# A hybrid convolution/attention network on one core: the bias table ahead of the first projection, filling products on the array, layer 1's weights prepared during the first image, and two edits in layer 1

## The chip, the core and the metric

The kernel runs on one core of a Trainium2 chip. The metric is the device time of one execution in microseconds. TensorE is called the array or PE here, VectorE DVE, ScalarE ACT, GpSimd POOL, and SyncE (which only issues transfers here) SP. ACT issues transfers too. Each engine takes its instructions in the order in which the program gives them, and each waits for what its own instructions need.

## The reference

Eight images of 384 channels and 32 x 32 positions (1024 tokens), all in float32, pass through two layers. Layer 0 is attention of 8 heads of 48 channels with a learnt bias for each relative position; layer 1 is attention of 6 heads of 64 channels and a feed-forward network with signed weights (computed for the first five images; the others get zero).

```python
# layer 0
rel = coords[:, None, :] - coords[None, :, :]          # over (31, 31)
hidden = gelu(rel @ mlp_w1 + mlp_b1)                   # 192 wide, exact gelu
bias = hidden @ mlp_w2 + mlp_b2                        # one per head and pair of positions
q, k, v = heads(groupnorm(x) @ qkv_w + qkv_b)
attn = softmax(q @ k.T * 48 ** -0.5 + bias)
x = x + (attn @ v) @ proj_w + proj_b
# layer 1
q, k, v = heads(layernorm(t) @ qkv_w.T)
q, k = normalize(q), normalize(k)                      # (t - mean) / std over a head's 64 channels
t = t + (softmax(q @ k.T * 64 ** -0.5) @ v) @ proj_w.T + proj_b
t = t + bitlinear(gelu(bitlinear(layernorm(t), W1, b1)), W2, b2)
```

The bias depends only on the difference of two positions, so 63 x 63 = 3969 values per head are all there is.

## The kernel before, in words

Everything is written out in program order by hand, image by image. Small pieces of work that are to run beside the main stream are given to a list (`later`): `later.after(n, work)` emits `work` after n further steps. In image 0 a step is taken after each of the six products of `project_qk` (three pairs of heads, q and k), after each of the four of `project_v`, and then after each of the 32 units of attention. So step 10 lies between the last product of `project_v` and unit 0.

**The order at the start.** `stages` are the pieces of the group norm of image 0: three measure the channels as they land and send the statistics to DRAM and back (`there`, `gs`), `stages[3]` makes scale and shift (`gsc`), `stages[4]` applies them on VectorE. `place_weights_qk` moves the q and k weights from a raw copy that lies in `grow` to their place. `hidden(r)` (r = 0, 1) makes the hidden layer of the bias network: four products `ph` of two rows each on the array (K = 2), each followed by a gelu on ACT. `table_part(r)` multiplies them by the second weights (`pb`, 16 records) and writes one half of the positions of the four groups to a table in DRAM (`table`). Before the change `table_part(0)` stands ahead of the first product of `project_qk`, and `table_part(1)` behind it.

**The bias parts.** `grow` holds the bias, spread out so that a score tile can read its own with one access pattern. It is filled in 32 parts, (head, quarter) in that order. `grow_loads` issues four transfers on SP for a part (`wide<-table`, or `oT<-table` for the parts from the 21st on, which use another buffer), 457 KB in all; `grow_turns` turns it round into `grow`, even quarters on ACT, odd ones on VectorE. The loads go out in lots of 3, 3, 3, 3, 2, 2, 2, 2 at steps 2 to 9, the turns at steps 3 to 6 and 8 to 11. So 18 turns stand ahead of unit 0 in the engines' queues, and one more comes at each step from 11 on. `wide` has the nine buffers of the tag `e`, which `rel` and the hidden tiles use first.

**A unit.** `scores` makes two tiles of scores on the array (L521, `s`), VectorE adds the bias to each (L532, "bias sum", two of 1.2 us), ACT takes the exponential (L536), and `weigh` multiplies by v two units later (L552, `o`). There are four PSUM tiles in all.

**Layer 1's first weights.** `_Start` loads them during image 7 of layer 0, takes the mean over the inputs with products of ones (`cm`, L146: 12 and 6 records), subtracts it on GpSimd, and then takes each head's mean out of q and k (`heads`).

**The end.** In the last image `divide` sums the exponentials of the last pair (`sum`, L1398), sends the sums through DRAM to spread them, inverts them and multiplies (L1434). `project_out` (`pp`, L1453) has done the first two pairs by then and waits for the third. Each third of the output is added on VectorE (L1458) and stored.

**Feed-forward images.** Behind attention the array makes the token sums `tsf` in the middle of the next image's first projection product, and `tsa` (the sums for the next image's norm) after it. `layer_norm` sends `lr` to DRAM and reads it back as `lc` and `ls`.

Of the kernel before, what the change touches and what calls it, by code (L numbers as in the profile page):

```python
# [19 lines left out]
F32 = mybir.dt.float32  # L20
# [100 lines left out]
class _Start:  # L121
# [4 lines left out]
    def __init__(self, tc, ins, x1, shared):  # L126
        self.nc, self.ins, self.x1, self.shared = tc.nc, ins, x1, shared

    def load_weights(self):
        self.wqkv = self.shared.weights("wqkv").rearrange("p (k c) -> p k c", k=KC)  # L130
        self.nc.sync.dma_start(
            self.wqkv, self.ins["L1_attn_qkv_wT"].rearrange("(k p) c -> p k c", p=P)
        )
# [5 lines left out]
    def means(self, temp, at, n):  # L139
        nc = self.nc  # L140
        pm = self.shared.mm2(f"cm{at}")
        for h in range(-(-n // HALF)):
            w = min(HALF, n - h * HALF)
            for k in range(KC):
                cols = slice(at + h * HALF, at + h * HALF + w)
                nc.tensor.matmul(  # L146
                    pm[:, h, :w], self.shared.ones, self.wqkv[:, k, cols],
                    start=(k == 0), stop=(k == KC - 1),
                )
        self.mean = temp(f"cmean{at}")  # L150
        nc.scalar.activation(
            self.mean[:, :n], pm.rearrange("p h q -> p (h q)")[:, :n], AF.Copy, scale=1.0 / C
        )

    def subtract(self, at, n):
        for k in range(KC):
            w = self.wqkv[:, k, at : at + n]
            self.nc.gpsimd.tensor_sub(w, w, self.mean[:, :n])

    def heads(self, k):  # L160
        nc = self.nc
        w = self.wqkv[:, k, 0 : 2 * C].rearrange("p (h d) -> p h d", d=D1)
        hm = self.shared.pool.tile([P, 2 * H1], F32, tag="hm", name=f"hm{k}")
        nc.vector.tensor_reduce(hm, w, AX.X, ALU.add)
        nc.gpsimd.tensor_scalar(hm, hm, 1.0 / D1, 1.0, ALU.mult, ALU.mult)
        nc.gpsimd.tensor_sub(w, w, hm.unsqueeze(2).to_broadcast([P, 2 * H1, D1]))

    def stages(self, temp):

        first, rest = (0, 2 * HALF), (2 * HALF, 3 * C - 2 * HALF)  # L170
        return [
            (5, self.load_weights),
            (6, self.load_image),
            (10, lambda: self.means(temp, *first)),
            (11, lambda: self.subtract(*first)),
            (12, lambda: self.means(temp, *rest)),
            (14, lambda: self.subtract(*rest)),
            (19, lambda: self.heads(0)),
            (21, lambda: self.heads(1)),
            (23, lambda: self.heads(2)),  # L180
        ]


def _layer0(tc, ins, x1, sums, shared, beside):
# [9 lines left out]
    with ExitStack() as ctx:  # L194
# [31 lines left out]
        QT, QN = 32, 2 * HALF  # L226
# [5 lines left out]
        nc.vector.memset(rel, 0.0)  # L232
        nc.vector.memset(w2, 0.0)
        nc.vector.memset(b2, 0.0)
        for g in range(P // QT):
            at = g * QN
            n = min(QN, NREL - at)
            nc.scalar.dma_start(rel[g * QT : g * QT + 2, 0:n], ins["rel"][:, at : at + n])
            nc.scalar.dma_start(w1[g * QT : g * QT + 2], ins["L0_conv_mlp_w1"])
        with nc.allow_non_contiguous_dma(reason="a bias, once"):  # L240
            nc.scalar.dma_start(b1, ins["L0_conv_mlp_b1"].rearrange("(k p) -> p k", p=HC))
            nc.scalar.dma_start(
                w2[:, :, 0:H0], ins["L0_conv_mlp_w2"].rearrange("(k p) h -> p k h", p=HC)
            )
        for g in range(P // QT):
            nc.scalar.dma_start(b2[g * QT : g * QT + H0], ins["L0_conv_mlp_b2"].unsqueeze(1))
# [8 lines left out]
        first = load(0)  # L255

# [31 lines left out]

        def place_weights_qk():
# [13 lines left out]
        def load_bias_qk():  # L303
            with nc.allow_non_contiguous_dma(reason="a bias, once"):
                for j in range(2):
                    for row, n, at, step in (
                        (j * S0, D0, j * D0, 2 * D0),
                        (j * S0 + D0, FR, (2 * NF0 + j) * D0, FR),
                    ):
                        for s in range(2):  # L310
                            nc.sync.dma_start(
                                bqk[row : row + n, s],
                                bass.AP(
                                    qkv_b.tensor, qkv_b.offset + s * C + at, [[1, n], [step, NF0]]
                                ),
                            )

        def load_weights_v_out():
            nc.sync.dma_start(wv, qkv_w[:, 2 * C : 3 * C].rearrange("(k p) c -> p k c", p=P))
            nc.sync.dma_start(bv, qkv_b[2 * C : 3 * C].partition_broadcast(P))  # L320
            pw = ins["L0_conv_proj_w"]
            for j in range(2):
                last = (2 * NF0 + j) * D0
                for row, n, at, step in (
# [3 lines left out]
                    nc.sync.dma_start(  # L328
# [5 lines left out]
                nc.sync.dma_start(wl[j * S0 + SP : (j + 1) * S0], pw[last : last + D0])  # L334
            with nc.allow_non_contiguous_dma(reason="a bias, once"):
                nc.sync.dma_start(bp, ins["L0_conv_proj_b"].rearrange("(k p) -> p k", p=P))
# [3 lines left out]
        WR = GW // 4  # L340

        def hidden(r):

            hids = {}
            for k in range(2):
                for a in range(2):
                    ph = mm2(f"ph{r}{k}{a}")
                    for i in range(2):
# [17 lines left out]
        def table_part(r, hids):  # L366
            pb = mm2(f"pb{r}")
            for k in range(2):
# [6 lines left out]
            nc.vector.tensor_scalar_add(backwards(part[:, HALF - 1 : HALF], HALF), pb[:, 0], b2)  # L375
            for g in range(P // QT):
                at = g * QN + r * HALF
                n = min(HALF, NREL - at)
# [264 lines left out]
        place_weights_qk()  # L643
        hids = [hidden(r) for r in range(2)]
        stages[3]()
        load_bias_qk()
        stages[4](nc.vector)
        load_weights_v_out()
        table_part(0, hids[0])
        later.after(1, lambda: table_part(1, hids[1]))  # L650
        nc.scalar.activation(tiny[:, 1:2], tiny[:, 0:1], AF.Exp)
# [14 lines left out]
        for i, n in enumerate((3, 3, 3, 3, 2, 2, 2, 2)):  # L666
            later.after(i + 3 + (i > 3), lambda n=n: grow_turns(n))
            later.after(i + 2, lambda n=n: grow_loads(n))
        for i in range(len(parts) - 20):
# [4 lines left out]
        with_last = beside(etile)  # L674
        for b in range(B):
            held = []
            for i, u in enumerate(units):
# [10 lines left out]
                if b == B - 1:  # L688
                    for at, work in with_last:
# [341 lines left out]
def _layer1(tc, ins, x1, out, shared, start, before=None, check=None):  # L1031
# [4 lines left out]
    with ExitStack() as ctx:  # L1036
# [405 lines left out]
        def project_out(b, oT, xt, then, between=None):  # L1442

            pps = []
            for pairs in (range(NP1 - 1), range(NP1 - 1, NP1)):
                if between is not None and NP1 - 1 in pairs:
                    between()
                for m in range(KC):
                    if len(pps) <= m:
                        pps.append(mm2(f"pp{b}_{m}"))  # L1450
                    for k in pairs:
                        for h in range(NH):
# [4 lines left out]
                    if NP1 - 1 in pairs:  # L1457
                        nc.vector.scalar_tensor_tensor(  # L1458
                            xt[:, m], flat2(pps[m]), bp[:, m : m + 1], xt[:, m], ALU.add, ALU.add
                        )  # L1460
                        then(m)

        def store(b, xt, k):
            nc.sync.dma_start(out[b, ts(k, P)].rearrange("p h w -> p (h w)"), xt[:, k])
# [404 lines left out]
```

## Time and profile before

| | |
|---|---|
| Median of three runs | 3040.62 us (3038.88 to 3041.24) |
| Profiled execution, its own time | 3043.66 us |
| Span of its instructions | 3041.8 us |
| PE / DVE / ACT / POOL busy | 3017.7 / 1769.1 / 1402.7 / 465.0 us |
| Mean granted clock of the array | 0.999 |
| Mean DMA rate | 49 GB/s |
| First product of `project_qk`, image 0 | 23.24 us |
| First scores, image 0 | 73.86 us |
| First product of `project_qk`, image 1 | 189.20 us |
| Last array record begins | in the group at 3029.19 us, 5.42 us long |

Times in the profile are microseconds from the start of the span. A line of the order of time gives start, length, engine, line of the program, operation, output<-input, shapes, how many were merged, and in brackets how long the engine was idle before and what ended it. A float32 product shows as two records. Rows of SPq or ACTq are issues of transfers, not the transfers. An array that is "busy" may still run at half its clock: the granted clock stands in the table by stretches, and the distance of records shows it as well.

### The profile page before, as it was taken

To read this page: it belongs to the slowest core of one execution; us is meant where nothing else is said; L and a number is where in the kernel's file an instruction comes from. 1 tells how busy PE (TensorE), PEld (TensorE's weight loads), DVE (VectorE), ACT (ScalarE), POOL (GpSimd) and SP (SyncE) were. 2 spreads that over 40 slices of the span, in tenths; PEclk is the share of its full clock that TensorE was granted. 3 is DMA by queue.
4 is the path that set the end of the run, shared out by engine and by line. 5 is a ranking of instruction groups with operands and counts; after the bars stand their busy time and mean duration, and the time that the engine had idled before them with its cause. 6 is when DMAs were issued, how large, how long until landed. Compare 5 with 4: busy or idle time off the path is not lost.

```text
span 3041.8 us, 45673 instructions
## 1 busy us (share of the span) xinstructions
PE 3017.7 (99%) x18914; PEld 1610.8 (53%) x18914; DVE 1769.1 (58%) x1760; ACT 1402.7 (46%) x1760; POOL 465.0 (15%) x315
## 2 busy tenths in 40 slices
PE   8999999999999999999999999999999999999998
PEld 3455546455554645444545655655655655645453
DVE  3746647373655727355565765765765755755545
ACT  2634526253443616244463553553653543654534
POOL 0111102021110202123202202202202202211110
PEclk9999999999999999999999999999999999999999
DMA  7412020211212020121411101101101101102011
GB/s 178 120 26 83 19 82 23 70 32 26 76 22 79 23 78 23 32 93 51 108 34 37 50 16 37 50 22 31 50 23 30 50 23 30 50 17 72 16 51 44
DMA packets 102449, 150.48 MB, mean 49 GB/s; under 512 B 59924, under 2 KB 63492, under 8 KB 101464
## 3 DMA queue, kind: packets, MB, share of 16 engines
q1 hardware_dynamic: 99368, 147.41, 17.3%
q8 instruction: 152, 2.49, 0.3%
q14 instruction: 65, 0.53, 0.1%
q10 hardware_dynamic: 2864, 0.05, 0.1%
HBM read 111.05 MB, written 27.32 MB: 45 GB/s over the span
## 4 chain that ended last, share of the span: by engine, by line
PE 93%; DMA 3%; DVE 3%; ACT 1%; SPq 1%; issue 0%; POOL 0%; ACTq 0%; DVEq 0%; POOLq 0%
PE s L521 15%; PE o L552 14%; PE s L1322 11%; PE o L1371 11%; PE pq L467 8%; PE pq L1178 6%; PE y2p L1593 6%; PE pp L616 4%; PE pv L1259 4%; PE y1p L1542 4%; PE pp L1453 4%; PE pv L495 4%; PE sum L1398 1%; DMA wide<-table 1%; PE hs L1207 1%; DVE lun L1494 1%
## 5 line engine op out<-in xcount | busy, mean ns | idle before, releaser
L536 ACT ACTIVATE e<-e 128x1024 f32<-128x1024 f32 x512 | 535.0, 1057 | 441.9 <-DVE e L532 422.0
L532 DVE TENSOR_TENSOR e<-s,grow 128x1024 f32<-128x1024 f32 x512 | 601.4, 1219 | 190.3 <-PE s L521 189.7
L521 PE MATMUL s<-qk 48*64 48x512 f32 x4096 | 613.5, 592 | 3.3 <-DVE e L532 3.2
L552 PE MATMUL o<-e,v 64*64 64x512 f32 x4096 | 607.5, 589 | 0.0
L1333 ACT ACTIVATE e<-s,kc 128x512 f32<-128x512 f32 x768 | 463.9, 694 | 172.2 <-PE s L1322 161.6
L1322 PE MATMUL s<-qk,qk 64*64 64x512 f32 x3072 | 418.6, 592 | 1.1 <-DVE oT L1381 0.9
L1371 PE MATMUL o<-e,v 64*64 64x512 f32 x3072 | 414.9, 590 | 0.0
L521 PEld LDWEIGHTS s<-qk 48*64 48x64 f32 x4096 | 237.4, 132 | 230.0 <-issue 76.7
L552 PEld LDWEIGHTS o<-e,v 64*64 64x64 f32 x4096 | 259.4, 133 | 178.5 <-issue 71.1
L1348 DVE TENSOR_TENSOR t<-t,e 128x1024 f32<-128x1024 f32 x192 | 231.0, 1222 | 53.4 <-ACT e L1333 53.3
L1178 PE MATMUL pq<-bx,wqkv 128*128 128x512 f32 x576 | 255.4, 596 | 0.7 <-ACT tra L1150 0.7
L1322 PEld LDWEIGHTS s<-qk,qk 64*64 64x64 f32 x3072 | 153.5, 132 | 191.5 <-issue 110.1
L467 PE MATMUL pq<-xn,w 128*128 128x512 f32 x576 | 251.6, 598 | 0.0
L1371 PEld LDWEIGHTS o<-e,v 64*64 64x64 f32 x3072 | 158.8, 133 | 169.9 <-issue 142.6
L581 POOL TENSOR_TENSOR inv<-sums,over 128x16 f32<-128x16 f32 x32 | 92.8, 2900 | 1009.7 <-DMA sums<-sd 851.0
L467 PEld LDWEIGHTS pq<-xn,w 128*128 128x128 f32 x576 | 109.5, 191 | 142.8 <-issue 140.3
L1178 PEld LDWEIGHTS pq<-bx,wqkv 128*128 128x128 f32 x576 | 107.4, 190 | 145.3 <-issue 141.5
L1345 DVE TENSOR_TENSOR t<-e,e 128x1024 f32<-128x1024 f32 x96 | 114.2, 1224 | 79.6 <-ACT e L1333 79.5
L1529 DVE TENSOR_REDUCE parts<-y 128x1 f32<-128x1024 f32 x75 | 90.1, 1217 | 93.3 <-ACT y L1526 92.7
L1228 POOL TENSOR_TENSOR hc<-hc,rsqrt 128x32 f32<-128x32 f32 x24 | 139.2, 5800 | 2.0
L1194 ACT ACTIVATE qsq<-pq 128x1024 f32<-128x1024 f32 x48 | 49.2, 1025 | 194.5 <-DVE qk L1188 105.8
L477 DVE TENSOR_SCALAR qk<-pq,bqk 128x1024 f32<-128x1024 f32 x24 | 30.8, 1284 | 177.1 <-PE pq L467 177.1
(161 smaller groups left out, 3026.9 us busy)
## 6 DMA issues: line engine op xcount, KB each, us to landing
rb<-rd SPq DMA_DIRECT2D x112, 256.0 KB
xn<-in_x_dram SPq DMA_DIRECT2D x24, 512.0 KB
res<-in_x_dram SPq DMA_DIRECT2D x24, 512.0 KB
x<-res SPq DMA_DIRECT2D x24, 512.0 KB
bx<-x SPq DMA_DIRECT2D x8, 1536.0 KB
rq<-hi SPq DMA_DIRECT2D x48, 256.0 KB
out_dram<-bx SPq DMA_DIRECT2D x24, 512.0 KB
wide<-table SPq DMA_DIRECT2D x80, 114.2 KB
```

Source lines behind the costliest of these rows:

```text
L467: nc.tensor.matmul(pq[:, h], wqk[:, k, s, 2 * pair : 2 * pair + 2, :].rearrange("p h d -> p (h d)"), xn[:, k, ts(h, HALF)], start=(k == 0) ...
L521: nc.tensor.matmul(s[j][ts(c, QP), i], qk[pair][rows, 1, ts(4 * m2 + 2 * i + c, QP)], qk[pair][rows, 0, ts(h, HALF)], start=True, stop=True,)
L532: nc.vector.tensor_add(e.rearrange("p (i q) -> p i q", i=2), s[j], bass.AP(near.tensor, near.offset, [near.ap[0], [-QROWS * IW, 2], [1, HA ...
L536: nc.scalar.activation(e, e, AF.Exp)
L552: nc.tensor.matmul(po[ts(j, S0), r], v[keys, 2 * m2 + i, 2 * pair + j, :], es[j][keys, ts(i, HALF)], start=(m2 == 0 and i == 0), stop=(m2 ...
L1178: nc.tensor.matmul(pq[:, h], wqkv[:, k, s * C + pair * P : s * C + (pair + 1) * P], xt[:, k, ts(h, HALF)], start=(k == 0), stop=(k == KC - 1),
L1228: nc.gpsimd.tensor_tensor(c, c, rsqrt.to_broadcast(list(c.shape)), ALU.pow)
L1322: nc.tensor.matmul(s[j][ts(c, QP), i], qk[pair, 1][rows, ts(4 * m2 + 2 * i + c, QP)], qk[pair, 0][rows, ts(h, HALF)], start=True, stop=True,)
L1333: nc.scalar.activation(e[:, ts(i, HALF)], s[j][:, i], AF.Exp, scale=kc[:, pair, j, m : m + 1])
L1348: nc.vector.tensor_add(total[j], total[j], e)
L1371: nc.tensor.matmul(po[ts(j, D1), r], v[keys, 2 * m2 + i, at : at + D1], es[j][keys, ts(i, HALF)], start=(m2 == 0 and i == 0), stop=(m2 == ...
L1593: nc.tensor.matmul(py[m][:, h], w2[:, k, ts(m, P)], supply.parts[k][i][:, ts(h, HALF)], start=(k == 0 and i == 0), stop=(k == FC - 1 and i ...
```

## The change

The change has three parts.

1. Image 0. Both table parts are emitted ahead of the first projection. The table's groups are 982, 982, 982 and 1023 positions wide instead of 1024, 1024, 1024 and 897, so `rel` and `w1` come in four transfers instead of eight and only one column of `rel` is cleared. `stir` puts products of ones into a free PSUM bank: seven ahead of the first `ph`, one ahead of each other `ph` and each `pb`, two behind the second `pb`. The second table part is evicted by ACT. `b1` is loaded by SP ahead of the raw weights, `w2` and `b2` by ACT after the gelu's table has been loaded by a tiny instruction. The biases of q and k and the weights for v and for the output move from SP's queue to ACT's, behind the table. The bias parts are loaded at steps 0 to 7 and turned at steps 2 to 5 and 7 to 10, so 20 turns stand ahead of unit 0. Layer 1's first weights come over ACT's queue into the room of the last three heads of `grow`; GpSimd adds their three chunks (step 2), three products of ones sum over the partitions (step 3), VectorE scales (step 4), GpSimd subtracts and takes out the heads' means (steps 4 to 8), and the result is stored to DRAM (step 9). In image 7 it is only loaded again.
2. The end. `divide_last` sums with 64 columns of ones, so that each partition of PSUM has its divisor; VectorE inverts from PSUM and multiplies. The last third of the output is added and stored in two halves. The loops of `project_out` over halves and pairs are exchanged.
3. `tsa` is emitted directly behind `tsf`.

```diff
+class _Weights:
+    def load(self, here, mean):
+        self.w = here.rearrange("p (k c) -> p k c", k=KC)
+        self.mean = mean
+        self.nc.scalar.dma_start(
+            self.w, self.ins["L1_attn_qkv_wT"].rearrange("(k p) c -> p k c", p=P)
         )
+    def add(self):
+        for k in range(1, KC):
+            self.nc.gpsimd.tensor_add(self.mean, self.w[:, 0] if k == 1 else self.mean, self.w[:, k])
+    def means(self):
...
+                self.nc.tensor.matmul(
+                    pm[:, h, :w], self.shared.ones, self.mean[:, cols], start=True, stop=True
+                )
...
+    def take(self):
+        for at, n, pm in self.sums:
+            self.nc.vector.tensor_scalar_mul(self.mean[:, at : at + n], pm[:, :n], 1.0 / C)
+    def subtract(self, k):
+        self.nc.gpsimd.tensor_sub(self.w[:, k], self.w[:, k], self.mean)
...
+    def store(self):
+        self.nc.sync.dma_start(self.ready, self.w.rearrange("p k c -> p (k c)"))
...
+        def stir(bank, n):
+            for _ in range(n):
+                nc.tensor.matmul(
+                    bank.rearrange("p (a b) -> p a b", b=P), shared.ones,
+                    shared.ones.unsqueeze(1).to_broadcast([P, HALF // P, P]), start=True, stop=True,
+                )
...
                     ph = mm2(f"ph{r}{k}{a}")
+                    stir(ph[:, 0], 1 if r or k or a else 7)
...
             pb = mm2(f"pb{r}")
+            stir(pb[:, 1], 1)
...
-            nc.vector.tensor_scalar_add(backwards(part[:, HALF - 1 : HALF], HALF), pb[:, 0], b2)
+            turned = backwards(part[:, HALF - 1 : HALF], HALF)
+            if r == 0:
+                nc.vector.tensor_scalar_add(turned, pb[:, 0], b2)
+            else:
+                stir(pb[:, 1], 2)
+                nc.scalar.activation(turned, pb[:, 0], AF.Identity, bias=b2)
...
         place_weights_qk()
+        nc.scalar.activation(tiny[:, 1:2], tiny[:, 0:1], AF.Gelu)
+        load_hidden_rest()
         hids = [hidden(r) for r in range(2)]
         stages[3]()
+        for r in range(2):
+            table_part(r, hids[r])
         load_bias_qk()
+        nc.scalar.activation(tiny[:, 1:2], tiny[:, 0:1], AF.Exp)
+        weights.load(*early)
+        load_weights_v_out()
         stages[4](nc.vector)
-        load_weights_v_out()
-        table_part(0, hids[0])
-        later.after(1, lambda: table_part(1, hids[1]))
-        nc.scalar.activation(tiny[:, 1:2], tiny[:, 0:1], AF.Exp)
+        for at, work in (
+            (2, weights.add), (3, weights.means), (4, weights.take), *(
+                (at + k, lambda k=k, work=work: work(k))
+                for at, work in ((4, weights.subtract), (6, weights.heads)) for k in range(KC)
+            ), (9, weights.store),
+        ):
+            later.after(at, work)
...
         for i, n in enumerate((3, 3, 3, 3, 2, 2, 2, 2)):
-            later.after(i + 3 + (i > 3), lambda n=n: grow_turns(n))
-            later.after(i + 2, lambda n=n: grow_loads(n))
+            later.after(i + 2 + (i > 3), lambda n=n: grow_turns(n))
+            if i == 0:
+                grow_loads(n)
+            else:
+                later.after(i, lambda n=n: grow_loads(n))
...
+        def divide_last(b, oT, pair):
...
+                    nc.tensor.matmul(
+                        pst[ts(j, D1), h], ones[:, 0:D1], folded[pair, j][:, ts(h, HALF)],
+                        start=True, stop=True,
+                    )
...
+                nc.vector.reciprocal(rb[:, cols], pst[:, h])
+                nc.vector.tensor_mul(oT[:, pair, cols], oT[:, pair, cols], rb[:, cols])
...
-                divide(b, oT, [NP1 - 1])
                 later.finish()
-                project_out(b, oT, xt, lambda m: store(b, xt, m))
+                divide_last(b, oT, NP1 - 1)
+                project_out(b, oT, xt, lambda m, cols: store(b, xt, m, cols), parts=NH)
...
-                    middle=lambda: fc.append(
-                        token_sums(f"f{b}", (xt[:, KC - 1], two), (fsq[KC - 1], fsq[0]))
-                    ),
-                )
+                    middle=lambda: fc.extend((
+                        token_sums(f"f{b}", (xt[:, KC - 1], two), (fsq[KC - 1], fsq[0])),
+                        token_sums(f"a{b + 1}", *ahead_sums),
+                    )),
+                )
+                tk = fc[1]
                 un, begin, normal = layer_norm(b, xt, fc[0])
-                tk = token_sums(f"a{b + 1}", *ahead_sums)
```

## The prediction

> **What bounds the kernel now.** First the shares of the engines, then what the array waited for. The array (PE) is busy nearly all the time; it waits 16.4 us in all and stands still for the last 7 us, after its last product. So a gain is array work taken out, or one of the few places where the array stands or runs slowly.
>
> ```profile
> PE 3017.7 (99%) x18914; PEld 1610.8 (53%) x18914; DVE 1769.1 (58%) x1760; ACT 1402.7 (46%) x1760; POOL 465.0 (15%) x315
> ...
> PE ph L350 <- DMA w<-in_L_conv_mlp_w_dram: 7.7, 2, 7.3
> PE s L521 <- DVE e L532: 3.2, 3, 2.2
> PE pp L1453 <- DVE oT L1434: 2.3, 1, 2.3
> ```
>
> Three places matter: the start, the bias in image 0 and the end. Next, the array in order of time (start, length, what):
>
> ```profile
> 19.67 3.64 PE L370 MATMUL pb<-hid,w 96*32 96x512 f32 x16
> 23.24 7.41 PE L467 MATMUL pq<-xn,w 128*128 128x512 f32 x12
> 30.58 1.92 PE L370 MATMUL pb<-hid,w 96*32 96x512 f32 x16
> ...
> 58.29 15.64 PE L495 MATMUL pv<-w,xn 128*128 128x384 f32 x48
> 73.86 4.53 PE L521 MATMUL s<-qk 48*64 48x512 f32 x32
> 80.57 4.67 PE L521 MATMUL s<-qk 48*64 48x512 f32 x16 [2.17 <-DVE e L532]
> ...
> 1337.80 5.42 PE L146 MATMUL cm<-wqkv,ones 128*128 128x512 f32 x12
> ...
> 1350.18 0.94 PE L146 MATMUL cm<-wqkv,ones 128*128 128x128 f32 x6
> ...
> 3029.19 5.42 PE L1453 MATMUL pp<-oT,L_attn_proj_wT 128*128 128x512 f32 x12 [2.32 <-DVE oT L1434]
> ```
>
> A 512-column f32 product is two records. In later images 72 of them take 31.10 us, 0.43 each; the first ones after 23.24 come 0.86 apart until 27.3. The slow clock costs 2 us there. The same 16 pb take 3.64 us at 19.67 and 1.92 at 30.58. Now VectorE, SyncE's transfers, and two stretches by engine (the last three numbers: granted clock, DMA share, GB/s):
>
> ```profile
> 78.73 0.65 DVE L403 COPY grow<-wide 128x480 f32<-128x480 f32 x1 [2.42 <-DMA wide<-table]
> 79.30 2.35 DVE L532 TENSOR_TENSOR e<-s,grow 128x1024 f32<-128x1024 f32 x2
> ...
> 86.92 0.65 DVE L403 COPY grow<-oT 128x480 f32<-128x480 f32 x1 [1.06 <-DMA oT<-table]
> 87.48 2.35 DVE L532 TENSOR_TENSOR e<-s,grow 128x1024 f32<-128x1024 f32 x2
> ...
> 35.02 5.40 SPq L391 DMA_DIRECT2D wide<-table  x12
> ...
> 55.02 10.22 SPq L391 DMA_DIRECT2D wide<-table  x20
> ...
> 75.00:80.00 5.00, 3.40 (x24) 0.85 (x16) 2.58 (x5) 0.59 (x1) 0.00 (x0) 1.00 1.05 236
> 80.00:85.00 5.00, 4.37 (x17) 1.06 (x21) 3.71 (x5) 2.86 (x4) 0.00 (x0) 0.69 0.79 214
> ```
>
> The scores at 73.86 come at once; their first bias sum (79.30) stands behind the 18th bias part. The parts come by DMA, saturated from 40 to 80 us: 20 issues in 10.22 us, four to a part, 2.04 us a part. From 73.86 to image 1's first projection (189.20) are 115.3 us; the like stretch of image 1 (239.57 to 363.65), less its output projection of 15.65, is 108.4. The bias costs image 0 6.9 us.
>
> [...]
>
> **The change part by part.** The profiled execution took 3043.66 us, 3.0 above the median of the runs; I sum differences and set them on the median, 3040.62.
>
> *Means of layer 1's weights.* In the chain of waits the 18 cm records take 5.35 + 0.87 = **-6.2**. Three products (six records, 2.0 us) come into image 0's projection; priced below.
>
> *The end.* The divisor now comes from PSUM. sum: 8 records, two side by side instead of four, 1.9 us for 1.1: +0.8. VectorE: a reciprocal took 0.245 us on 16 columns and 0.346 on 32, so 512 would be about 3.4; two of them and two multiplies of 0.69 end near 3025, before the first 24 pp records do (10.4 us, 3027.5). That hides them; without it 2.3 stays. The wait of 2.32 goes and with it the switch. -1.9. The last sum is split: its second half ends 0.3 us earlier. **-2.2** (0 to -3).
>
> *tsa beside tsf in the five FFN images.* One switch of tile shape less (8 hs or tsa records take 1.00, not 0.86): **-0.7** (0 to -1). Its two transfers pass layer_norm's on SP, but tra is ready 6 us before lr is.
>
> *Reordered pp loop, Gelu and Exp tables loaded by hand.* Same counts; 0.
>
> *The start.* Seven ones products, 14 records, from 1.0 us: six at 0.86 until the clock is released [...], eight at 0.43: 9.6. rel and w1 have landed by then (7.3 and 10.5 before, issued later and in eight pieces). Each ph is 0.86 plus a ones product 0.86 plus switches, 1.9: seven more end at 23.7, so TensorE, not the gelu (1.02 each), sets the pace. Then ones, pb0, ones, pb1, two ones: 0.9 + 1.85 + 0.9 + 1.85 + 1.7 = 7.2. The projection starts at **30.9** instead of 23.24, but warm and without the 1.92 of pb1. gsc (18.66) and apply are hidden behind this, as are table_part(0)'s eviction ahead of apply on VectorE. It ends, with the three products, at 64.0 instead of 58.29; scores at 79.7 instead of 73.86.
>
> *Queues.* load_bias_qk (8 issues) and load_weights_v_out (10) leave SP, where they went out from 17.2 to 25.4, for ACT, behind pb1's eviction: with weights 19 issues of 0.45, so ACT issues from about 30 to 39. Its next work is the eviction of the second projection product at 41; bqk lands by 36, when VectorE evicts the first; wv is needed at 64. Hidden, with 2 us to spare at the closest; beyond that the four PSUM tiles give a product's length (5.2) more. On SP b1 goes ahead of the raw weights, which still land with the same bytes before them, near 10.3. ACT issues w2 and b2 ahead of the first gelu, by about 8: hidden behind the ones products.
>
> *The bias parts.* pb1 is evicted at 29.8; parts start 1.6 us after that as before (33.4, 35.02): **31.4** instead of 35.0. But now 20 parts stand ahead of the first bias sum, and ACT's queue moves in the same time wv, bv, wp, wl, bp (which took 6 us of the DMA between 22 and 30, when it was else idle) and the 1.77 MB of layer 1's weights (at the 350 GB/s of 1316-1322, 5 us). Ahead of part 22, SP issues store, another 5 us. Before: 18 parts x 2.04 = 36.7 of 43.7 us; the other 7.0 (qk rows, first landing) stay. If all adds up: 31.4 + 40.8 + 7.0 + 6 + 5 = 90.2, then two parts and store, 99.3 against 86.92: **+12.4**. If ACT's transfers and store slip wholly between: 79.2, before the scores (79.7) need it; the third bias sum then follows the array, 80.7 + 2 x 3.44 (a unit) = 87.6, as before: **0**. No row decides: the 3656-byte packets kept the DMA at share 1.0 but moved only 236 GB/s. I take the middle, **+6.2**.
>
> *Waits added.* The three products wait for GpSimd: weights land about 12 us after the projection's start, two adds of 2.7 us (2.38 for 1024 columns) end at 48 to 50, the array is there at 46.4. Up to 4 us and some slow clock; behind it the rest of the projection. Hidden if the parts are late, else 0 to +5; I take 0. Subtractions, heads and store (GpSimd 18 us, VectorE 5) end near 75, before SP reaches store.
>
> Sum: -6.2 - 2.2 - 0.7 + 6.2 = -2.9, so **3038**; own range 3034 to 3045.
>
> **Rivals.** *The transfers interleave.* For it: the packets took 0.25 us at 236 GB/s where other loads moved 400. [...] Image 0 costs 0 to +2: 3031 to 3034, **3032**.
>
> *The clock falls back during the table (slower).* ones and ph alternate; [...] each of seven pairs +1.7, pb and their ones +5, the table 17 us later and the parts with it: 6.2 + 17 - 9.1 = +14, **3055**. [...]
>
> *It doesn't do what it says*: "pauses" don't exist, since ph plus ones is longer than a gelu. That is in the forecast.
>
> **How the numbers follow.** Forecast 0.47, interleaved 0.27, clock or a like delay 0.26. About 0.2% (6 us) is what a measurement of this kernel can tell from no change. The forecast lies within it but for its edges; the first rival is below, the second above: faster 0.29, same 0.44, slower 0.27. Range 3030 to 3053.
>
> **What would show it.** No cm near 1340; no wait at the last pp; ones to about 9.6; projection from about 31 at 0.43 a record; first part issued near 31; third bias sum between 90 and 96. Wrong: that sum at 88 (interleaved) or past 105 (clock), a granted clock below 1 before 30, or an array gap at the three products above 5 us.

## The result, and the profile after

The changed kernel takes **3063.34 us**, median of four runs (3057.36 to 3066.19), against 3040.93 for the kernel before on the same chip: ratio 1.0069, 95% interval 1.0056 to 1.0082. It is 22 us slower, and above the predicted range. The profiled execution took 3063.18 us with a span of 3061.4, 19.6 more than before (whose profiled execution was itself 2.7 us above its median).

The array's waits, longest sums first:

```profile
PE s L554 <- DVE e L565: 4.6, 2, 3.3
PE cm L148 <- POOL grow L138: 4.3, 1, 4.3
...
PE pq L500 <- ACT qk L514: 1.2, 1, 1.2
```

The wait for `rel` and `w1` (7.7 us) and the one at the last `pp` (2.3) are gone; 4.3 us at the three products of ones on the weights' sum are new. All its waits together are 14.9 us, against 16.4 before, so the loss isn't mainly in waits. The array in order of time (start, length, what):

```profile
1.01 8.70 PE L363 MATMUL ph<-ones 128*128 128x512 f32 x14 [1.01 <-POOL ones L109]
9.65 1.10 PE L377 MATMUL ph<-rel,w 2*96 2x512 f32 x4
10.68 1.12 PE L363 MATMUL ph<-ones 128*128 128x512 f32 x2
11.73 1.10 PE L377 MATMUL ph<-rel,w 2*96 2x512 f32 x4
12.77 2.07 PE L363 MATMUL ph<-ones 128*128 128x512 f32 x2
14.77 2.02 PE L377 MATMUL ph<-rel,w 2*96 2x512 f32 x4
...
38.53 2.66 PE L398 MATMUL pb<-hid,w 96*32 96x512 f32 x16
...
45.85 15.61 PE L500 MATMUL pq<-xn,w 128*128 128x512 f32 x36
65.75 4.21 PE L148 MATMUL cm<-grow,ones 128*128 128x512 f32 x6 [4.29 <-POOL grow L138]
69.75 5.83 PE L500 MATMUL pq<-xn,w 128*128 128x512 f32 x12
76.79 10.57 PE L500 MATMUL pq<-xn,w 128*128 128x512 f32 x24 [1.20 <-ACT qk L514]
...
102.77 4.05 PE L554 MATMUL s<-qk 48*64 48x512 f32 x32
```

The same two ones records take 1.12 us at 10.68 and 2.07 at 12.77, the same four `ph` 1.10 and 2.02: the clock was released and fell again, two banks into the table. It returns inside the first `pb` (2.66 lies between 3.64 and 1.92). The table by stretches of the array's slow clock (after the engines: granted clock, DMA share, GB/s):

```profile
12.80:40.00 27.20, 27.20 (x48) 6.26 (x50) 2.85 (x7) 7.77 (x7) 1.25 (x4) 0.50 0.01 1
64.00:70.70 6.70, 4.95 (x8) 2.37 (x9) 1.84 (x2) 2.19 (x3) 1.69 (x1) 0.50 0.99 189
```

The array is busy for all of the first stretch, at half clock; the second is the wait for POOL with what follows it. Behind them the other engines, VectorE first, then SP, ACT and POOL:

```profile
108.29 0.65 DVE L436 COPY grow<-wide 128x480 f32<-128x480 f32 x1 [3.56 <-DMA wide<-table]
108.86 4.61 DVE L565 TENSOR_TENSOR e<-s,grow 128x1024 f32<-128x1024 f32 x4
116.06 0.65 DVE L436 COPY grow<-oT 128x480 f32<-128x480 f32 x1 [2.59 <-DMA oT<-table]
```
```profile
48.62 30.11 SPq L424 DMA_DIRECT2D wide<-table  x36
```
```profile
67.59 1.11 ACT L514 ACTIVATE qk<-pq,bqk 128x1024 f32<-128x1024 f32 x1 [16.16 <-DMA wp<-in_L_conv_proj_w_dram]
```
```profile
60.40 5.30 POOL L138 TENSOR_TENSOR grow<-grow 128x1152 f32<-128x1152 f32 x2 [42.49 <-DMA grow<-in_L_attn_qkv_wT_dram]
```

Nine parts were asked for in 30 us. The 20th part is turned at 108.29, 59.7 us after the first was issued; the scores, ready from 102.77, wait for it. ACT computed nothing for 16 us ahead of its eviction of the second projection product, because the issues of weight loads stood in its queue; the product itself was done near 56, so the eviction came some 11 us late. The end of the program, the array and then VectorE:

```profile
3036.77 1.94 PE L1492 MATMUL sum<-f,ones 128*64 128x512 f32 x8
3038.64 15.72 PE L1513 MATMUL pp<-oT,L_attn_proj_wT 128*128 128x512 f32 x36
```
```profile
3042.78 3.35 DVE L1499 RECIPROCAL rb<-sum 128x512 f32<-128x512 f32 x1
3046.16 0.69 DVE L1500 TENSOR_TENSOR oT<-oT,rb 128x512 f32<-128x512 f32 x1
```

36 `pp` records run without a break; the division ends at 3046.85, ahead of the 25th record at 3049.

Where the 19.6 us of span are, by the start of the same work in both traces: image 1's projection at 218.28 against 189.13 (189.20 in the table above), **+29.2**; layer 1's at 1461.79 against 1439.67, so **-7.0** between them (the `cm` products); the last `sum` 3036.77 against 3015.22, **-0.6** in layer 1's images; the end **-2.0**. Image 0 alone is the loss.

### The profile page after: what moved, and what is told of

It is laid out like the page before. It is cut to its first block, busy times and chain, and to the rows that moved or that the text cites. A ratio compares the mean times of both kernels' runs of the same rounds, so it can differ in the third digit from the quotient of the medians.

```text
span 3061.4 us, 45718 instructions
## 1 busy us (share of the span) xinstructions
PE 3039.2 (99%) x18938; PEld 1606.2 (52%) x18938; DVE 1775.5 (58%) x1764; ACT 1402.6 (46%) x1759; POOL 469.1 (15%) x314
## 3 DMA queue, kind: packets, MB, share of 16 engines
q10 hardware_dynamic: 5472, 3.35, 0.5%
## 4 chain that ended last, share of the span: by engine, by line
PE 92%; DMA 3%; DVE 3%; SPq 1%; ACT 1%; POOL 1%; issue 1%; ACTq 0%; DVEq 0%; POOLq 0%
PE s L554 14%; PE o L585 14%; PE s L1367 11%; PE o L1416 11%; PE pq L500 7%; PE y2p L1659 5%; PE pq L1223 5%; PE pp L649 4%; PE pv L1304 4%; PE y1p L1608 4%; PE pp L1513 4%; PE pv L528 4%; PE sum L1443 1%; PE ph L363 1%; DMA wide<-table 1%; SPq L424 1%
## 5 line engine op out<-in xcount | busy, mean ns | idle before, releaser
L585 PEld LDWEIGHTS o<-e,v 64*64 64x64 f32 x4096 | 251.9, 133 | 186.8 <-issue 90.1
L1416 PEld LDWEIGHTS o<-e,v 64*64 64x64 f32 x3072 | 158.0, 133 | 170.7 <-issue 143.4
L1304 PE MATMUL pv<-wqkv,bx 128*128 128x384 f32 x384 | 131.9, 497 | 0.0
```

Source lines behind the costliest of these rows:

```text
L585: nc.tensor.matmul(po[ts(j, S0), r], v[keys, 2 * m2 + i, 2 * pair + j, :], es[j][keys, ts(i, HALF)], start=(m2 == 0 and i == 0), stop=(m2 ...
L1304: nc.tensor.matmul(pv[:, i, 0:C], xt[:, k].rearrange("c (p m) -> c m p", m=MT)[:, 2 * m2 + i], wqkv[:, k, 2 * C : 3 * C], start=(k == 0), ...
L1416: nc.tensor.matmul(po[ts(j, D1), r], v[keys, 2 * m2 + i, at : at + D1], es[j][keys, ts(i, HALF)], start=(m2 == 0 and i == 0), stop=(m2 == ...
```

## The experiments

The kernel before ran between 3041.7 and 3042.5 (medians) beside these. Edits are to the kernel after unless said otherwise.

**The parts in layer 1 alone** (`e4_ends_only`): the kernel before with `divide_last`, the reordered `pp` loop, the halves of the last sum, and `tsa` beside `tsf`. For the end:

```diff
-                divide(b, oT, [NP1 - 1])
                 later.finish()
-                project_out(b, oT, xt, lambda m: store(b, xt, m))
+                divide_last(b, oT, NP1 - 1)
+                project_out(b, oT, xt, lambda m, cols: store(b, xt, m, cols), parts=NH)
```

> The kernel before with the changes of layer 1 alone: the end without the way through DRAM, the last third in two halves, the loops of project_out exchanged, tsa behind tsf. By the working of the prediction -2.2 for the end and -0.7 for tsa: 3038. Rival for tsa (its records are a cost that moves, not one that goes): -2.2 only.

Measured: 3038.17 us, ratio 0.9988 (0.9981 to 0.9995). A gain of 3.5 us, as expected; these parts aren't the loss.

**No products of ones** (`e1_no_ones`).

```diff
-            for _ in range(n):
+            for _ in range(0):
```

> The changed kernel without any product of ones. Theory A (the front is long because ones and ph alternate and the clock falls: 27.3 us at half clock in the changed kernel): without ones the array follows the gelus, 1.02 us each, about 10.5 to 18.7; pb0 and pb1 3.6 us each at half clock, to about 26; the projection starts near 26 instead of 45.85 and is slow for its first 4 us. Parts start near 29 instead of 48.6, the 20th is turned near 88, image 0 as a whole is some 20 us shorter than in the changed kernel: about 3041 to 3044. Theory B (the loss is made by the transfers and the products' wait behind the table, whatever the array does before it): only the time of the ones themselves goes, and the kernel stays above 3055.

Measured: 3042.93 us, 1.0005 (0.9996 to 1.0013): some 20 us less than after. The array's order of time shows more than the clock:

```profile
8.23 8.25 PE L377 MATMUL ph<-rel,w 2*96 2x512 f32 x32 [8.23 <-DMA w<-in_L_conv_mlp_w_dram]
16.41 5.41 PE L398 MATMUL pb<-hid,w 96*32 96x512 f32 x32
21.77 15.70 PE L500 MATMUL pq<-xn,w 128*128 128x512 f32 x36
42.71 4.21 PE L148 MATMUL cm<-grow,ones 128*128 128x512 f32 x6 [5.25 <-POOL grow L138]
```

Its clock is released only at 20.0 (1.00 from 20.1 on), yet eight banks of `ph` (a bank here is one PSUM tile with its four records) take 8.25 us, 1.03 each: as long as one bank took in after at **full** clock (9.65 to 10.68), and half of its 2.0 at half clock. The gelus keep the same time (eight in 8.12 us), so this pace may be theirs as much as the array's. In before, too, no ones stand between the banks, and there two `ph` records of one bank and two of the next start within 0.06 us (15.66 to 15.72). In after two start at 9.65 and the other two of the same bank at 10.15. A ones product of 128 rows, put between the banks, would part them, and so cost `ph` its overlap even with the clock held: that was my estimate from these starts, and the next two runs test it.

**Two ones for one** (`e2_two_ones`), ahead of each `ph` but the first and ahead of each `pb`.

```diff
-                    stir(ph[:, 0], 1 if r or k or a else 7)
+                    stir(ph[:, 0], 2 if r or k or a else 7)
...
-            stir(pb[:, 1], 1)
+            stir(pb[:, 1], 2)
```

> The changed kernel with two products of ones instead of one ahead of each ph after the first and each pb. Theory A1 [...] the clock stays released from 6 us on, a pair takes 2.8 us instead of 3.96 at half clock, and the projection starts at about 39 although 9 products more are made: 3053 to 3058. Theory A2 (small products end the released state whatever stands between them): a pair takes 5.7 us, the projection starts near 60: 3075 to 3085.

Measured: 3059.82 us, 1.0056 (1.0041 to 1.0071).

```profile
10.52 1.99 PE L363 MATMUL ph<-ones 128*128 128x512 f32 x4
12.44 1.10 PE L377 MATMUL ph<-rel,w 2*96 2x512 f32 x4
...
40.50 15.61 PE L500 MATMUL pq<-xn,w 128*128 128x512 f32 x36
```

Every bank takes 1.10, and the granted clock is 1.00 from 12.8 to 40: it holds throughout the table. The projection still starts at 40.50: a bank is now 1.92 + 1.03. Holding the clock in this way costs most of what it brings: the run is 3.5 us less than after, and 1.8 above the range of theory A1.

**The same ones in pairs** (`e6_ones_paired`).

```diff
-                    stir(ph[:, 0], 1 if r or k or a else 7)
+                    stir(ph[:, 0], 7 if not (r or k or a) else 0 if a else 2)
```

> After, with the same number of ones products less one, but two of them ahead of every second bank of the hidden layer instead of one ahead of each, so that the hidden layer's products of two banks follow each other. Theory O (the ones products between the banks also part products that otherwise run four at a time[...]): two banks take about 1.1 us together at full clock, the hidden layer ends near 20 and, if the clock holds as it did with two ones, the projection starts near 27 instead of 45.9: 3044 to 3047. Rival (only the clock mattered; side by side gives nothing): two banks take 2.1, the projection starts at 31 with the clock held: 3048 to 3051. If the clock falls all the same: a start at 36 or later, 3053 to 3060.

Measured: 3046.36 us, 1.0012 (1.0006 to 1.0019).

```profile
10.10 1.11 PE L377 MATMUL ph<-rel,w 2*96 2x512 f32 x8
11.14 1.98 PE L363 MATMUL ph<-ones 128*128 128x512 f32 x4
...
27.66 15.61 PE L500 MATMUL pq<-xn,w 128*128 128x512 f32 x36
```

Eight `ph` records take what four took (1.11 us), so the lost overlap is shown. The clock held here too (1.00 from 12.8 to 40), and so the two effects have to be told apart: with one ones product fewer than after, the table is 18.2 us shorter and the run 17 us. Of the 18.2, four pairs of banks make some 4 us and the product less 1. The rest is the clock: with the lengths at full clock (a bank 1.03, a product of ones 1.05, `pb` 1.86) after's projection would have started near 32.9, by this estimate, instead of 45.85, 13 us earlier. Ones took 1.92 of 2.96 us here and 1.92 of 2.94 with two, against 1.05 of 2.08 in after.

**The products of the weights' sum later** (`e10_means_later`).

```diff
-            (2, weights.add), (3, weights.means), (4, weights.take), *(
+            (2, weights.add), (5, weights.means), (6, weights.take), *(
...
-                for at, work in ((4, weights.subtract), (6, weights.heads)) for k in range(KC)
-            ), (9, weights.store),
+                for at, work in ((6, weights.subtract), (7, weights.heads)) for k in range(KC)
+            ), (10, weights.store),
```

> The kernel after with the three products of ones on the weights' sum two steps later (behind the fifth block of the projection instead of the third, and what follows them one to three steps later), so that the sum, done at 65.7, is not waited for. Everything else as in after, so the clock falls in the table as it did. Theory (the wait of 4.3 us is only the first to be met of several that late transfers bring; [...] and the biases' 20th turn stood until 108.3): PE waits for ACT in place of POOL, by 4 to 6 us, and the third bias sum stays at 114 to 118: 3060 to 3065. Rival (the wait and the slow stretch behind it are a cost of their own): 7 to 9 us less than after, 3054 to 3057.

Measured: 3060.96 us, 1.0064 (1.0048 to 1.0079).

```profile
72.71 0.49 PE L148 MATMUL cm<-grow,ones 128*128 128x128 f32 x2 [2.93 <-ACT qk L514]
...
86.68 2.16 PE L528 MATMUL pv<-w,xn 128*128 128x384 f32 x3 [2.76 <-ACT qk L514]
```

The wait for POOL turned into 5.7 us for ACT, whose evictions now stood in its queue behind turns that waited for their bias parts. The wait for POOL was only the first to be met: from the projection's start to image 1's it took 173.2 us here and 172.4 in after, so moving the products gained nothing.

In this execution the clock held the same alternation until 18.6 us (12.8 in after), though nothing was changed ahead of it. The ones' own time just before a fall can be compared, over 3.4 us each (the shortest stretch at half clock in before, from 81.9 to 85.3, lasts that long). The first number behind the comma is the time of the ones' records in the last 3.4 us before the clock fell, in after and then in `e3`:

```profile
9.34:12.76 3.42, 1.50 (x3) 0.30 (x2) 1.00 0.36 107
```
```profile
9.77:13.18 3.41, 1.49 (x4) 0.50 (x4) 1.00 0.38 120
```

and in this run in two such stretches that kept the clock and in the one before the fall:

```profile
8.34:11.76 3.42, 2.00 (x5) 0.34 (x3) 1.00 0.80 282
11.76:15.17 3.41, 1.94 (x4) 0.59 (x4) 1.00 0.08 13
15.17:18.58 3.41, 1.49 (x4) 0.35 (x3) 1.00 0.01 1
```

So the clock fell three times behind 3.4 us with 1.49 or 1.50 of ones (0.44), and it held through two with 2.00 and 1.94 (0.57). With two ones and with pairs, where it held too, some 1.92 us of ones stand in each 2.94 or 2.96. The alternation in after has half on average, but a pair takes 2.08 us, and 3.4 us hold one product of ones and as much of the next as their start happens to leave. What share in what time decides the clock, these five stretches don't show.

**The transfers early, ones kept** (`e3_loads_early`): biases, layer 1's weights, `wv`, `bv`, `wp`, `wl`, `bp` go out on SP behind `gsc`, while the table is made (their issues change from `nc.scalar` to `nc.sync`, which the lines below leave out).

```diff
         stages[3]()
+        load_bias_qk()
+        weights.load(*early)
+        load_weights_v_out()
         for r in range(2):
             table_part(r, hids[r])
-        load_bias_qk()
...
-        weights.load(*early)
-        load_weights_v_out()
```

> The changed kernel with the biases of q and k, layer 1's weights and the weights for v and the output issued on SP behind gsc (about 20 us, when the DMA is idle) instead of on ACT behind pb1. Theory A (the transfers stand in one line with the bias parts and add up): the 20 parts take 48 us instead of 59.7, the three products find their sums ready (4.3 us of wait and 3.4 us of the second slow stretch go), scores near 95.5 instead of 102.8 and first bias sum near 97 instead of 108.9: 3050 to 3053. Rival (the transfers interleave and cost the parts nothing; the DMA of the parts is bound by its own source): only the products' wait goes, behind the parts, and the kernel stays at 3060 to 3063.

Measured: 3047.63 us, 1.0018 (1.0011 to 1.0025), below the range of theory A; in the profiled execution the clock fell as in after (records of 2.0 us from 13 to 40). One of the 18 executions took 3037.64 us with a mean granted clock of 0.999, the others 3044.8 to 3051.3 with 0.995 to 0.997. A mean of 0.999 leaves room for less than 10 us at half clock in all, so in that one execution the clock can't have been lost for 27 us, in the same kernel.

```profile
61.53 2.10 PE L148 MATMUL cm<-grow,ones 128*128 128x512 f32 x6
```
```profile
97.01 0.64 DVE L436 COPY grow<-wide 128x480 f32<-128x480 f32 x1
```

No wait at the sum, no second slow stretch, and the 20th turn comes 48.5 us after the first read (48.53) instead of 59.7. The other runs fall into the same two groups. With the loads among the table reads: 60.0 without ones, 61.7 with two, 61.4 with pairs, 61.2 with the sum later. With the loads ahead: 48.1 and 48.4 (`e5`, `e11`, below). The transfers add up: from the projection's start to image 1's it took 158.7 us here, and 172.4 in after.

**No ones and early transfers** (`e5_no_ones_early`): as `e1`; weights, `wv` and `bv` on SP behind `gsc`, biases on ACT behind the gelus, the rest on ACT behind the table.

```diff
-            for _ in range(n):
+            for _ in range(0):
...
-        self.nc.scalar.dma_start(
+        self.nc.sync.dma_start(
             self.w, self.ins["L1_attn_qkv_wT"].rearrange("(k p) c -> p k c", p=P)
...
         stages[3]()
+        load_bias_qk()
+        weights.load(*early)
+        load_weights_v_out()
         for r in range(2):
             table_part(r, hids[r])
-        load_bias_qk()
+        load_weights_out()
```

> The whole change without any product of ones, and with the transfers of the first image that the kernel after issues behind the table put where the queues are idle: the 8 biases on ACT between the last gelu and the second part, layer 1's weights and wv and bv on SP behind gsc, wp, wl and bp on ACT behind the table's second part. Theory (the loss is the ones products and the wait for the late weights; the rest of the change is a gain): the projection starts at about 21.8 us as without ones, there is no wait for POOL at the three products and no slow stretch behind it, so the scores start at about 71.7 (73.9 before) and layer 1 no longer makes its sums (7.0 us less between the images' start and layer 1's), and the end gives 2.2: 3041.7 - 2.1 - 7.0 - 2.3 = 3030, with the scores' own waits for biases at most 2 us shorter: 3027 to 3032. Rival (the transfers collide wherever they are put, with the statistics' small transfers or with the table's stores): projection or first table reads some 5 us later, 3035 to 3040.

Measured: **3034.74 us**, 0.9976 (0.9966 to 0.9986): faster than both kernels, by 7.6 us than before, but 5 short of the theory. On ACT and then on the array:

```profile
17.32 12.18 ACTq L329 DMA_DIRECT2D bqk<-in_L_conv_qkv_b_dram  x6
29.62 0.69 ACT L410 ACTIVATE part<-pb,b 128x512 f32<-128x512 f32 x1 [11.29 <-DMA bqk<-in_L_conv_qkv_b_dram]
```
```profile
49.56 13.51 PE L502 MATMUL pq<-xn,w 128*128 128x512 f32 x24 [4.33 <-ACT qk L516]
```

The bias issues took 12.18 us behind the big loads, which SP had issued from 19.80 on, so the table's second part was evicted at 29.6 (22.0 in `e1`), the bias parts came later, and PE waited 4.3 us for an eviction that stood on ACT behind a part's turn. That is what the rival had named, and the time is just below its range (3035 to 3040).

**Weights in layer 1** (`e7_weights_in_layer1`): `e5` with layer 1's weights made as in the kernel before.

```diff
-        weights.load(*early)
...
-        for at, work in (
-            (2, weights.add), (3, weights.means), (4, weights.take), *(
...
+        with_last = beside(etile)
```

> The kernel with no ones and early transfers (e5), but with layer 1's weights made where the kernel before makes them, beside the last image of layer 0: the first image has no weights to load, add, multiply or store. If the weights' move is worth what its own rows say (three products of 0.7 us each in the first image against the 7.0 us that layer 1 loses), this is 4.9 us slower than e5: 3033 to 3036. Rival (the table ahead is the gain and the weights in the first image cost as much as they save): equal to e5 within 1 us.

Measured: 3038.04 us, 0.9986 (0.9980 to 0.9993), 3.3 slower than `e5`: nearer the theory (4.9) than to equal, though 2 us outside the theory's range (3033 to 3036). Image 1's projection starts at 188.92, as before (189.13): the table ahead gains nothing in image 0, even without ones or weights. Almost all of this run's 4.3 us is what `e4` has.

**Seven ones ahead, none later** (`e8_seven_early`): `e5` with the first seven kept.

```diff
-                    stir(ph[:, 0], 1 if r or k or a else 7)
+                    stir(ph[:, 0], 0 if r or k or a else 7)
...
-            stir(pb[:, 1], 1)
...
-                stir(pb[:, 1], 2)
```

> e5 with seven ones products ahead of the first bank of the hidden layer and none later. The clock is released at about 6 us, and the question is whether the hidden layer's products of 2 rows hold it. If they don't count (theory of the clock): it falls at about 13 as in after, the table runs at half clock from there, and the projection starts 1 to 2 us later than in e5 and partly at half clock: 1 to 8 us slower than e5. If they do: the hidden layer runs at full clock, the eight gelus of 1.1 us set the pace, the projection starts at 20.5 and 0 to 3 us are gained on e5.

Measured: 3034.58 us, 0.9975 (0.9965 to 0.9985), the same as `e5`.

```profile
8.87 1.97 PE L379 MATMUL ph<-rel,w 2*96 2x512 f32 x16
11.18 5.03 PE L379 MATMUL ph<-rel,w 2*96 2x512 f32 x16 [0.34 <-ACT hid L384]
```
```profile
11.20:21.40 10.20, 10.20 (x44) 2.90 (x48) 4.38 (x10) 6.93 (x7) 1.25 (x4) 0.50 0.20 41
```

At full clock 16 records take 1.97 us; then the clock is at half from 11.2 on, 2.3 us after the last ones product, in an array that stood still for only 0.34. Products of two rows alone didn't hold the clock here. The theory of the clock held, but not its price: the first half at full clock made up for the later start, and the projection starts at 22.31, as in `e5` (22.45).

**The big loads on POOL's queue** (`e9_pool_queue`): no ones; weights, `wv` and `bv` issued by POOL, the biases where after has them.

```diff
-        self.nc.scalar.dma_start(
+        self.nc.gpsimd.dma_start(
             self.w, self.ins["L1_attn_qkv_wT"].rearrange("(k p) c -> p k c", p=P)
...
         stages[3]()
+        weights.load(*early)
+        load_weights_v_out()
         for r in range(2):
```

> No product of ones, as in e5, but layer 1's weights, wv and bv are issued on POOL's queue behind the small products of the statistics, and the 8 biases stay on ACT behind the table's second part, as in the kernel after. In e5 ACT stood 11.3 us for the completion of transfers ahead of a bias issue, so that the second part of the table came at 29.6 instead of 22.0 and ACT's first eviction at 38; PE then waited 4.3 us for an eviction and the clock fell for 6.8 us. Theory [...]: with the big loads on another queue ACT isn't held, the second part comes at 22, the first wide read at 28 to 30, PE doesn't wait in the projection, scores start at 72 and the third bias sum at 87 or before: 3027 to 3031. Rival (the bytes are what counts: the same loads and table reads have to pass before the 20th turn, whatever the queue): the third bias sum stays at 90 or later and the time within 2 us of e5, 3033 to 3036.

Measured: 3039.35 us, 0.9992 (0.9985 to 0.9998). A miss: 4.6 slower than `e5`. VectorE shows why:

```profile
27.41 4.56 DVE L483 TENSOR_SCALAR xn<-xn,gsc 128x1024 f32<-128x1024 f32 x3 [6.43 <-DMA gsc<-back]
```

The loads went out 3 us earlier than in `e5` and ahead of the statistics' last small transfers, which landed late; the projection started at 28.4. The second part was evicted at 22.7, as the theory had it.

**The biases first** (`e11_biases_first`): `e5` with the biases on SP between the statistics' transfers (diff against `e5`; their issues also change from `nc.scalar` to `nc.sync`).

```diff
+        load_bias_qk()
         hids = [hidden(r) for r in range(2)]
         stages[3]()
-        load_bias_qk()
```

> e5 with the 8 bias loads on SP between the statistics' first small transfers and the last two, ahead of the big loads, so that ACT isn't held by them between the gelus and the second part of the table. Theory ([...] the second part of the table at 29.6 instead of 22, PE waiting 4.3 us for an eviction, 6.8 us at half clock): the second part comes at 22, first wide read at 30, no wait of PE over 2 us in the projection, scores at 72 to 73, third bias sum at 85 to 88, the second image's projection at 188 to 190 instead of 194: 3029 to 3032. Rival (the table reads set the end of the first image whatever happens before them, as in the kernel with the weights in layer 1): the scores wait for the biases instead and the second image's projection stays at 192 or later: 3033 to 3036.

Measured: 3035.37 us, 0.9978 (0.9969 to 0.9986), as `e5`: the rival held. The second part was evicted at 22.5, but its stores took SP until 32.0 behind the big loads, the first read went out at 32.2, and the scores, ready at 75.3, waited for the bias:

```profile
80.57 0.65 DVE L438 COPY grow<-wide 128x480 f32<-128x480 f32 x1 [2.77 <-DMA wide<-table]
```

Image 1's projection starts at 191.4. In all five kernels with the loads ahead of the table reads and without ones between the products, the 20th part is turned between 79.9 and 82.5; nothing tried here brought it forward.

## Why the prediction was wrong

The likeliest case (3038) was not the one that came; the rival *the clock falls back during the table* (3055, given 0.26) was, and it came **with** the full cost of the transfers, not instead of it.

- ***The start* failed.** The projection was to start at 30.9 and started at 45.9, 15.0 later; the rival's own working said 17. The step took the clock as held, on my estimate that half of the time in full-array work would do. Half is the average: the last 3.4 us before each of the three falls held 1.49 or 1.50 us of ones (0.44). Once lost, the clock did not come back while 2.08 us of 3.41 (0.61) were ones at half clock (16.2 to 19.6 and 19.6 to 23.0 in after), and the loss lasted 27.3 us. The fall is worth some 13 of the 15 us, by the estimate under `e6`; the other 2 are mostly pairs of 2.08 us that were priced at 1.9.
- **A second fault in the same step** was not seen at all: pricing a bank at full clock by itself, not by what two banks take side by side without ones between them (1.11 us in `e6`, where one took 1.10 in after). This turns "ones cost some filler time and warm the array" into a loss even with the clock held: the projection starts at 27.7 with pairs (`e6`) and at 21.8 without ones (`e1`).
- ***The bias parts* failed in the choice, not the working.** The two ends were "all adds up", +12.4, and "interleave", 0; I took the middle, 6.2, for want of a row. The extra transfers were put at 6 + 5 = 11 us ahead of the 20th part; moving them away took 11.2 (59.7 to 48.5). From the first read to the 20th turn I had 58.8 at this end and the trace has 59.7. The third bias sum would have been at 99.3 + 15 = 114.3 with the late start; its part was turned at 116.1.
- ***Waits added* and *Queues* failed in part.** The three products waited 4.3 us (I had named up to 4 and taken 0), with 6.8 us at half clock behind it. ACT's eviction of the second projection product, priced with 2 us to spare, stood until 67.6 behind issues of loads (ACT idle for 16.16 us, ended by the transfer of `wp`). By itself the wait is worth little: with the sum later (`e10`) the time can't be told from that of after, since other waits take its place.
- ***Means* and *the end* were right**: -7.0 against -6.2 (the stretch from image 1 to layer 1 takes 1243.5 us in all ten traces with the weights in image 0 and 1250.3 to 1250.5 in the three without) and -2.0 against -2.2; a reciprocal of 512 columns took 3.35, the estimate was 3.4, and it was hidden. ***tsa beside tsf* is not settled**: from layer 1's first product to the last `sum` it took 1575.6 us before and between 1573.0 and 1576.0 in the twelve traces with the edit, so the -0.6 in after, close to the -0.7 predicted, may be luck.
- **Interleaving rival**: refuted by the 59.7 us. **"Doesn't do what it says"**: in a sense true. There were no pauses to fill; without the products the banks took as long at half clock (1.03 us each) as with them at full.

With the right branches the prediction's own sum was -9.1 + 12.4 + 17 = +20.3, or 3061. The range ended at 3053 because the clock and the full addition were taken as one case or the other, while a table that ends later pushes the additions back whole.

## What to carry to other kernels

Before putting filler products into a stream of small ones, look at how many of these start together: here a filler on all 128 rows ended that overlap, and the clock it kept paid back only what was lost (1.03 us a bank without it at half clock, 1.03 with it at full). Where a clock is to be held, look at the least share of work in a short stretch as well as the average: half on average was 0.44 in the 3.4 us before each fall. When two unfavourable mechanisms act on the same chain one after the other, add them before fixing the upper end of a range. Move a transfer into a stretch in which the DMA is idle (a share of 0.01 from 12.8 to 40 here), not only onto another queue, and see which small transfer or store then stands behind it.

## What was not expected of the hardware

- Eight banks of two-row products took 8.25 us at half clock without ones; one bank with ones between took 2.0 at half clock, 1.03 at full: side-by-side running was worth about the factor of two of the clock.
- The clock fell in an array that was busy all the time (27.20 of 27.20 us from 12.8 to 40.0 in after, granted 0.50): with half of the time in full products on average and 0.44 in the 3.4 us before the fall, and, in `e8`, with two-row products alone, 2.3 us after the last full one (0.50 from 11.2 to 21.4). A row of the profile that says busy did not mean a full clock.
- Issues of transfers stood for long on their engine, and what followed them there stood too: eight bias issues took 3.8 us on ACT in after, and six of them 12.18 in `e5` behind big loads that SP had issued; SP's eight stores took 6.2 us in after and 11.3 in `e11`. In `e5` the trace puts the end of ACT's 11.29 idle us ahead of the second part down to the transfer of the biases. In `e9`, with the big loads on POOL's queue, ACT's second part came at 22.7; but there the biases were issued behind it, so what held the issues was not tried by itself.
